# Graph layer: one unit in 60 fetched row by row on SyncE's queue

## The chip, the cores and the metric

The kernel runs on one core of a Trainium2 chip. The time is the device time of that core in microseconds, the median of three runs: 16161.78 us (16160.94 to 16164.18). Times in the profile come from one profiled execution of the same program, times of single instructions in nanoseconds where marked.

## The reference

A layer of a graph network on N = 50,000 nodes with 160 features (64 scalars and 32 vectors of 3) and 1,650,000 edges. The edges come sorted by destination. Each edge has a source, a destination and four numbers sh.

```
ss, vv = s[src], v[src]                       # rows of x, gathered by source
dot  = einsum('eui,ei->eu', vv, e1)           # e0 = sh[:, 0:1], e1 = sh[:, 1:4]
out0 = C0 * (ss * e0 @ W1 + dot * INV3 @ W2)
out1 = C1 * (p3 + p4 + p5)                    # products of ss, vv, cross(vv, e1) with e0, e1, W3, W4, W5
m_agg = segment_sum(concat(out0, out1), dst)  # summed over the edges of a destination
h    = m_agg's two parts @ Ws, Wv             # scaled
x    = layernorm(x + (x + relu(h)))
```

All of it is linear in the gathered row up to the relu. So the kernel sums, for each destination and each of the four numbers, (number x gathered row) first, and applies one combined weight matrix of 4 x 160 by 160 afterwards.

## The kernel before

The edges are cut into units of 128 edges: 12,891 of them, 12,894 with the padding. Six units are a group (G = 6): its destinations fit into a window of 32 slots (W = 32). There are 2149 groups. Two groups are a pair (PG = 2, 12 units), four groups a chunk whose 4 x 32 slots fill 128 partitions, and 20 groups a super-chunk (SG = 20, 120 units, 10 pairs); there are 108 super-chunks, the last with 9 groups.

`load` (L186 to L206) fetches a super-chunk's indices `ri` and edge numbers `ra` on SyncE's (SP's) queue at L193, L194 and L195, one unit to a partition. ScalarE (ACT) turns the indices into floats at L197, TensorE (PE) transposes them (L200, L205) so that an edge is on its own partition, and VectorE (DVE) writes the sources back as integers `si` (L202). `place` (L208 to L217) subtracts each group's first destination. Loads are made one super-chunk ahead.

`group_sums` (L219 to L242) handles a pair. GpSimd (POOL) issues one indirect DMA per unit, L225: 128 rows of x of 640 bytes each, one to a partition, into a part of the tile `xg`; 12 such parts make a tile, and there are 8 tiles (`rows`, bufs=8). DVE makes one-hot matrices times edge numbers (`hot` L230, `ha` L233). PE multiplies `ha` with the gathered rows, six units accumulating into one group's sums `ps` (L238), and ACT copies `ps` to `A` (L241).

`apply_weights` (L244 to L268) transposes a chunk's sums (L253), multiplies with the weights (L263) and leaves the rows `hp` (L267). `block` (L270 to L287) collects the chunks that touch a block of 128 nodes: SP loads the block's own rows `xt` (L275, 3 buffers), ACT doubles them (L277), PE gathers the chunks with a one-hot matrix (L286), and `norm` (L143 to L156) does relu, residual and layer norm and stores `out` on ACT's queue (L156). There are 391 blocks.

The main loop (L318 to L334) goes over the pairs: a load of the next super-chunk at the first pair of one, `group_sums`, then the chunk and the blocks that became complete a pair ago. Each engine works its own queue in order; the tile framework sets that order and puts in the waits, and a buffer of a pool is given out again when its last reader is done. What follows the loop checks that the windows held all edges, and a second path after it (L372 on, loops of zero turns on these inputs) would redo the work otherwise.

Of the kernel before, what the change touches and what calls it, by code (L numbers as in the profile page):

```python
# [29 lines left out]

F32 = mybir.dt.float32
I32 = mybir.dt.int32
AF = mybir.ActivationFunctionType
ALU = mybir.AluOpType
AX = mybir.AxisListType
ET = mybir.EngineType
PSUM = bass.MemoryType.PSUM

P = 128
MUL0, MUL1 = 64, 32  # L40
D = MUL0 + 3 * MUL1
# [10 lines left out]
QG = P // W  # L52
PG = 2
SG = 20


def plan(n_nodes, n_edges):

    nblk = 125
    assert n_nodes % nblk == 0  # L60
    nb = n_nodes // nblk
    again = 9

    per_unit = P * n_nodes / n_edges
    group = max(g for g in range(1, 17)
                if g == 1 or g * per_unit + 1 + 5 * math.sqrt(g * per_unit * per_unit / P) <= W)
    ngroups = math.ceil(math.ceil(n_edges / P) / group)
    units = P * math.ceil(max(math.ceil(n_edges / P) + again - 1, QG * math.ceil(ngroups / QG) * group) / P)
    return nblk, nb, again, group, units, ngroups
# [3 lines left out]
def tile_gnn_resnorm(ctx: ExitStack, tc: tile.TileContext, x, src, dst, attr, W1, W2, W3, W4, W5, Ws, Wv, out, n_edges):  # L73
    nc = tc.nc
    N = x.shape[0]
    NBLK, NB, GA, G, NU, NG = plan(N, n_edges)
# [14 lines left out]
    BWb = const.tile([D - P, NK, D], F32, name="BWb")  # L91
    more = const.tile([1, 2], I32, name="more")

    src1 = src.rearrange("(e o) -> e o", o=1)
    dst1 = dst.rearrange("(e o) -> e o", o=1)

    def weights(wp, psum):
# [45 lines left out]
    def norm(pool, ph, x2, n, row):  # L143
# [7 lines left out]
        rstd = pool.tile([P, 1], F32, name="rstd")  # L151
        nc.scalar.activation(rstd[:n], mv[:n, 1:2], AF.Sqrt, bias=eps_t[:n])  # L152
        nc.vector.reciprocal(rstd[:n], rstd[:n])  # L153
# [15 lines left out]
    alive = max(bs[-1] - bs[0] for bs in of_block) + 1  # L169
    NSC = math.ceil(NG / SG)  # L170

    with tc.tile_pool(name="once", bufs=1) as once, tc.tile_pool(name="raw", bufs=2) as rawp, \
            tc.tile_pool(name="idx", bufs=2) as idxp, tc.tile_pool(name="rows", bufs=8) as rowp, \
            tc.tile_pool(name="ops", bufs=3) as op, tc.tile_pool(name="sums", bufs=4) as sump, \
            tc.tile_pool(name="hp", bufs=alive + 3) as hpp, tc.tile_pool(name="node", bufs=3) as np_, \
            tc.tile_pool(name="psC", bufs=1, space=PSUM) as psC, tc.tile_pool(name="psK", bufs=2, space=PSUM) as psK, \
# [9 lines left out]
        def load(s):  # L186

            n = (min(NG, (s + 1) * SG) - s * SG) * G
            u0 = s * SG * G
            e = slice(u0 * P, (u0 + n) * P)  # L190
            ri = rawp.tile([P, 2, P], I32, name="ri")
            ra = rawp.tile([P, P, NK], F32, name="ra")
            nc.sync.dma_start(ri[:n, 0, :], src1[e].rearrange("(u p) o -> u (p o)", p=P))  # L193
            nc.sync.dma_start(ri[:n, 1, :], dst1[e].rearrange("(u p) o -> u (p o)", p=P))  # L194
            nc.sync.dma_start(ra[:n].rearrange("u p k -> u (p k)"), attr[e].rearrange("(u p) k -> u (p k)", p=P))  # L195
            rf = rawp.tile([P, 2, P], F32, name="rf")
            nc.scalar.copy(rf[:n], ri[:n])  # L197
            pi = psI.tile([P, 2, P], F32, name="pi")
            for i in range(2):
                nc.tensor.transpose(pi[:, i, :n], rf[:n, i, :], ident[:n, :n])  # L200
            si = idxp.tile([P, P], I32, name="si")
            nc.vector.tensor_copy(si[:, :n], pi[:, 0, :n])  # L202
            pk = psK.tile([P, NK, P], F32, name="pk")
            for k in range(NK):
                nc.tensor.transpose(pk[:, k, :n], ra[:n, :, k], ident[:n, :n])  # L205
            return s, n, si, pi, pk  # L206

        def place(loaded):  # L208

            s, n, si, pi, pk = loaded  # L210
            rel = idxp.tile([P, P], F32, name="rel")
            nc.vector.tensor_tensor(
                rel[:, :n].rearrange("p (g j) -> p g j", j=G), pi[:, 1, :n].rearrange("p (g j) -> p g j", j=G),
                baseB[:, s * SG:s * SG + n // G].unsqueeze(2).to_broadcast([P, n // G, G]), op=ALU.subtract)
            nc.vector.tensor_reduce(extremes[:, 0, s:s + 1], rel[:, :n], axis=AX.X, op=ALU.min)
            nc.vector.tensor_reduce(extremes[:, 1, s:s + 1], rel[:, :n], axis=AX.X, op=ALU.max)
            return si, rel, pk  # L217

        def group_sums(placed, u, ng):  # L219

            si, rel, pk = placed
            n = ng * G
            xg = rowp.tile([P, PG * G, D], F32, name="xg")
            for j in range(n):
                nc.gpsimd.indirect_dma_start(  # L225
                    out=xg[:, j, :], out_offset=None, in_=x,
                    in_offset=bass.IndirectOffsetOnAxis(ap=si[:, u + j:u + j + 1], axis=0))

            hot = op.tile([P, PG * G, W], F32, name="hot")
            nc.vector.tensor_tensor(hot[:, :n], slotsP[:, 0:W].unsqueeze(1).to_broadcast([P, n, W]),  # L230
                                    rel[:, u:u + n].unsqueeze(2).to_broadcast([P, n, W]), op=ALU.is_equal)
            ha = op.tile([P, PG * G, NK, W], F32, name="ha")
            nc.vector.tensor_tensor(ha[:, :n], hot[:, :n].unsqueeze(2).to_broadcast([P, n, NK, W]),  # L233
                                    pk[:, :, u:u + n].rearrange("p k u -> p u k").unsqueeze(3)
                                    .to_broadcast([P, n, NK, W]), op=ALU.mult)
            ps = psA.tile([P, PG, D], F32, name="ps")
            for j in range(n):
                nc.tensor.matmul(ps[:, j // G, :], ha[:, j].rearrange("p k w -> p (k w)"), xg[:, j, :],  # L238
                                 start=j % G == 0, stop=j % G == G - 1)
            A = sump.tile([P, PG, D], F32, name="A")  # L240
            nc.scalar.copy(A[:, :ng], ps[:, :ng])  # L241
            return A, ng  # L242

        def apply_weights(pairs):  # L244
# [3 lines left out]
            for f0, f1 in ((0, P), (P, D)):  # L248
                pt = psM.tile([P, QG, P], F32, name="pt", tag="misc")
                g = 0  # L250
                for A, n in pairs:
                    for i in range(n):
                        nc.tensor.transpose(pt[:f1 - f0, g, :], A[:, i, f0:f1], ident)  # L253
                        g += 1
# [15 lines left out]
        def block(b, hps):  # L270
# [15 lines left out]
                nc.tensor.matmul(ph[:nb], hot2[:r, i, :nb], hp[:r], start=i == 0, stop=i == len(cs) - 1)  # L286
            norm(np_, ph[:nb], x2[:nb], nb, row)  # L287

        loaded = {0: load(0)}


        base_d = dram.tile([NGP, 1], I32, name="base_d")
        with nc.allow_non_contiguous_dma(reason="one number of each group"):
            nc.sync.dma_start(base_d, dst1[0:NGP * G * P].rearrange("(g e) o -> g (e o)", e=G * P)[:, 0:1])
        baseI = once.tile([P, NGP], I32, name="baseI")
        nc.sync.dma_start(baseI, base_d.rearrange("g o -> o g").to_broadcast([P, NGP]))
# [3 lines left out]
        for g in range(QG):  # L300
            r = slice(g * W, (g + 1) * W)
# [4 lines left out]
        placed = {0: place(loaded.pop(0))}  # L306
# [10 lines left out]
        g = 0  # L317
        while g < NG:  # L318
            s = g // SG
            if g % SG == 0 and s + 1 < NSC:  # L320
                loaded[s + 1] = load(s + 1)
            ng = min(PG, NG - g, (s + 1) * SG - g)
            got = group_sums(placed[s], (g - s * SG) * G, ng)
            if ready:
                second(*ready.pop())
            pairs.append(got)
            g += ng
            if g % QG == 0 or g == NG:
                ready.append((c, pairs))
                pairs, c = [], c + 1  # L330
            if g % SG == 0 and g < NG:
                placed[s + 1] = place(loaded.pop(s + 1))
                del placed[s]
# [3 lines left out]
        far = once.tile([P, NCH], F32, name="far")  # L337
# [25 lines left out]
    mm_d = dram.tile([2, NU], F32, name="mm_d")  # L363
    tab_d = dram.tile([2, NB], I32, name="tab_d")
    tab = const.tile([1, 2, NB], I32, name="tab")
# [7 lines left out]
    with tc.tile_pool(name="up", bufs=1) as up, tc.tile_pool(name="us", bufs=2) as us, tc.For_i(0, once_more, 1):  # L373
# [16 lines left out]
        far = up.tile([PB, 2, CB, nseg], F32, name="far2")  # L390
        for s in range(nseg):
# [7 lines left out]
            for c in range(CB):  # L399
# [3 lines left out]
                at = us.tile([PB, 2, SEG], F32, name="at")  # L403
# [5 lines left out]
        f = up.tile([PB, CB], F32, name="f")  # L409
# [12 lines left out]
    with tc.tile_pool(name="edges2", bufs=2) as ep, tc.tile_pool(name="ops2", bufs=2) as op, \  # L422
# [3 lines left out]
        with tc.For_i(0, blocks, 1) as b:  # L426
# [5 lines left out]
            with tc.For_i(u0, u1, GA) as u:  # L432
                u = nc.s_assert_within(u, 0, NU - GA, skip_runtime_bounds_check_because="below u1")
# [9 lines left out]
                xg = op.tile([P, GA, D], F32, name="xg2")  # L443
# [10 lines left out]
                ps = psA.tile([NBLK, 2, 512], F32, name="ps2")  # L454
# [7 lines left out]
            for f0, f1 in ((0, P), (P, D)):  # L462
# [3 lines left out]
                at = np_.tile([f1 - f0, NK, NBLK], F32, name=f"ac{f0}")  # L466
# [3 lines left out]
            i = 0  # L470
# [4 lines left out]
            row = ds(b * NBLK, NBLK)  # L475
# [37 lines left out]
```

## Time and profile before

| what | value |
|---|---|
| median of three runs | 16161.78 us |
| the profiled execution's own time | 16161.21 us |
| its span, first to last instruction | 16159.5 us |
| granted TensorE clock | 0.662 |
| gathers (L225) | 12894, 945 ns each |
| gathers' DMA queue | 618912 packets, 1057.10 MB, 26.6% of the 16 DMA engines |
| SP's DMA queue | 102084 packets, 72.77 MB, 1.6% |
| issue of `xt` on SP (L275), min/median/max | 327/351/616 ns, 1.9 us to landing |
| issue of `ri` (L193, L194) and `ra` (L195), median | 347, 403 and 347 ns |
| CAST of the indices on ACT (L197) | 398 ns |
| load of one register on SP (TENSOR_LOAD, L359), two of them | 290 and 475 ns |

"Busy" is the time in which an engine executes instructions; register, semaphore and DMA-issuing instructions are left out of it, so SP has no row. "Idle before, releaser" tells what the engine waited for ahead of an instruction; "issue" means that it waited for nothing that the profile shows. The time of a DMA instruction on SP is the time in which SP is occupied with it, and "to landing" runs from the issue to the arrival of the data.

### The profile page before, as it was taken

How to read it: one execution, taken by the hardware profiler on the slowest of the kernel's cores; microseconds unless marked ns; L12 is line 12 of the kernel's file. 1: busy time of each engine (PE TensorE's matmuls, PEld its weight loads, DVE VectorE, ACT ScalarE, POOL GpSimd, SP SyncE). 2: the span in 40 equal slices, each digit the busy share in tenths (PEclk: the TensorE clock that was granted, in tenths of full speed). 3: DMA queues.
4: the chain of work that ended last, by engine and by line, in shares of the span. 5: the costliest groups of instructions: out<-in, count | busy, mean ns of one | idle time of the engine just before them, and what ended most of it. 6: DMA issues, size and time to landing. Idle time of an engine off the chain costs nothing. (4 is left out here: it accounts for less than half of the span.)

```text
span 16159.5 us, 115933 instructions
## 1 busy us (share of the span) xinstructions
PE 13061.2 (81%) x43943; PEld 9172.6 (57%) x43944; DVE 3450.3 (21%) x5361; ACT 1521.6 (9%) x3583; POOL 12192.5 (75%) x12905
## 2 busy tenths in 40 slices
PE   7878888878888887888888888888788888887887
PEld 5555555555555555555555555555555555555555
DVE  2222222222222222222222222222222222222221
ACT  1000000000000000000000000000000000000000
POOL 7777777777777777777777777777777777777776
PEclk6666666666666666666666666666666666666666
DMA  3222222222222222222222222222222222222222
GB/s 79 73 72 72 73 73 72 72 73 72 72 73 72 72 73 73 72 73 72 73 72 73 72 73 72 73 72 72 73 72 73 72 72 72 73 73 72 72 71 65
DMA packets 778423, 1169.89 MB, mean 72 GB/s; under 512 B 226314, under 2 KB 558406, under 8 KB 777732
## 3 DMA queue, kind: packets, MB, share of 16 engines
q0 software_dynamic: 618912, 1057.10, 26.6%
q1 hardware_dynamic: 102084, 72.77, 1.6%
q10 hardware_dynamic: 56864, 32.58, 0.7%
q8 instruction: 346, 5.67, 0.1%
q14 instruction: 217, 1.78, 0.0%
HBM read 1129.30 MB, written 32.25 MB: 72 GB/s over the span
## 5 line engine op out<-in xcount | busy, mean ns | idle before, releaser
L225 POOL DMA_INDIRECT xg<-in_x,si x12894 | 12190.9, 945 | 3933.3 <-issue 3793.9
L238 PE MATMUL ps<-xg,ha 128*128 128x160 f32 x25788 | 8965.8, 457 | 3056.3 <-DMA xg<-in_x,si 2998.2
L238 PEld LDWEIGHTS ps<-xg,ha 128*128 128x128 f32 x25788 | 5534.5, 267 | 6130.7 <-DMA xg<-in_x,si 5458.9
L233 DVE TENSOR_TENSOR ha<-hot,pk 128x1536 f32<-128x1536 f32 x1075 | 1884.7, 1753 | 10801.5 <-PE ps L238 10801.5
L263 PE MATMUL phc<-BWb,at 32*128 32x160 f32 x4304 | 1624.9, 471 | 0.0
L241 ACT COPY A<-ps 128x320 f32<-128x320 f32 x1075 | 456.8, 425 | 11583.8 <-PE ps L238 11569.5
L253 PE MATMUL pt<-ident,A 128*128 128x128 f32 x4298 | 1361.4, 394 | 0.4 <-ACT at L256 0.4
L286 PE MATMUL phb<-hp,hot 128*128 128x160 f32 x4584 | 1349.4, 483 | 0.0
L286 PEld LDWEIGHTS phb<-hp,hot 128*128 128x128 f32 x4584 | 1202.2, 331 | 129.0 <-issue 129.0
L263 PE MATMUL phc<-BWa,at 128*128 128x160 f32 x4304 | 1262.7, 386 | 0.0
L263 PEld LDWEIGHTS phc<-BWb,at 32*128 32x128 f32 x4304 | 892.6, 256 | 557.2 <-issue 556.7
L263 PEld LDWEIGHTS phc<-BWa,at 128*128 128x128 f32 x4304 | 1026.0, 270 | 0.4 <-DVE st L148 0.2
L253 PEld LDWEIGHTS pt<-ident,A 128*128 128x128 f32 x4298 | 750.1, 175 | 104.8 <-ACT at L256 0.8
L256 ACT COPY at<-pt 128x512 f32<-128x512 f32 (+1 forms) x1076 | 623.2, 579 | 1137.6 <-PE pt L253 1137.4
L230 DVE TENSOR_TENSOR hot<-slotsP,rel 128x384 f32<-128x384 f32 x1075 | 597.0, 556 | 31.4
L281 DVE TENSOR_TENSOR hot<-slotsP,rr 128x768 f32<-128x768 f32 (+2 forms) x391 | 362.9, 928 | 0.0
L146 DVE SCALAR_TENSOR_TENSOR y<-phb,x 128x160 f32<-128x160 f32 x391 | 126.9, 325 | 800.3 <-PE phb L286 800.3
L277 ACT ACTIVATE x<-xt 128x160 f32<-128x160 f32 x391 | 131.6, 337 | 1341.7 <-DVE y L146 1341.2
L202 DVE CAST si<-pi 128x120 int32<-128x120 f32 x108 | 30.4, 282 | 882.9 <-DMA xg<-in_x,si 879.7
L267 ACT COPY hp<-phc 128x160 f32<-128x160 f32 x538 | 157.3, 292 | 195.0 <-PE phc L263 194.9
L155 DVE TENSOR_SCALAR o<-y,mv,rstd 128x160 f32<-128x160 f32 x391 | 149.2, 382 | 14.1
L152 ACT ACTIVATE rstd<-mv,eps_t 128x1 f32<-128x1 f32 x391 | 115.2, 295 | 334.3 <-DVE mv L150 329.6
(67 smaller groups left out, 856.0 us busy)
## 6 DMA issues: line engine op xcount, KB each, us to landing
xg<-in_x,si POOLq DMA_INDIRECT x12894, 2.6
xt<-in_x SPq DMA_DIRECT2D x390, 80.0 KB, 1.9
out<-o ACTq DMA_DIRECT2D x390, 80.0 KB, 1.7
ra<-in_attr SPq DMA_DIRECT2D x107, 240.0 KB, 3.0
ri<-in_src SPq DMA_DIRECT2D x107, 60.0 KB, 2.0
ri<-in_dst SPq DMA_DIRECT2D x107, 60.0 KB, 2.0
baseI<-base_d SPq DMA_DIRECT2D x1, 1076.0 KB, 7.5
BVd<-BV ACTq DMA_DIRECT2D x1, 240.0 KB
```

Of the source, the lines that this page charges most:

```text
L155: nc.vector.tensor_scalar(o[:n], y[:n], mv[:n, 0:1], rstd[:n], op0=ALU.subtract, op1=ALU.mult)
L225: nc.gpsimd.indirect_dma_start(out=xg[:, j, :], out_offset=None, in_=x, in_offset=bass.IndirectOffsetOnAxis(ap=si[:, u + j:u + j + 1], axi ...
L230: nc.vector.tensor_tensor(hot[:, :n], slotsP[:, 0:W].unsqueeze(1).to_broadcast([P, n, W]), rel[:, u:u + n].unsqueeze(2).to_broadcast([P, n ...
L233: nc.vector.tensor_tensor(ha[:, :n], hot[:, :n].unsqueeze(2).to_broadcast([P, n, NK, W]), pk[:, :, u:u + n].rearrange("p k u -> p u k").un ...
L238: nc.tensor.matmul(ps[:, j // G, :], ha[:, j].rearrange("p k w -> p (k w)"), xg[:, j, :], start=j % G == 0, stop=j % G == G - 1)
L241: nc.scalar.copy(A[:, :ng], ps[:, :ng])
L253: nc.tensor.transpose(pt[:f1 - f0, g, :], A[:, i, f0:f1], ident)
L256: nc.scalar.copy(at[:, :, :ng].rearrange("f k g w -> f g k w"), pt[:f1 - f0, :ng].rearrange("f g (k w) -> f g k w", w=W))
L263: nc.tensor.matmul(ph[:ng * W], at[:, k, :ng].rearrange("f g w -> f (g w)"), bw[:, k, :], start=i == 0, stop=i == 2 * NK - 1)
L267: nc.scalar.copy(hp[:ng * W], ph[:ng * W])
L281: nc.vector.tensor_tensor(hot2[:, :len(cs)], slotsP.unsqueeze(1).to_broadcast([P, len(cs), P]), rr[:, :len(cs)].unsqueeze(2).to_broadcast( ...
L286: nc.tensor.matmul(ph[:nb], hot2[:r, i, :nb], hp[:r], start=i == 0, stop=i == len(cs) - 1)
```

## The change

In pairs 4 and 9 of each super-chunk the twelfth unit is no longer gathered by POOL. Its 128 rows are fetched by SP with 128 DMAs of one row each, into a tile `xr` of its own (a pool of 3 buffers). For the addresses ACT makes a tile `ro` of byte offsets (source x 640) from the loaded indices, still one unit to a partition, and SP reads 32 of them at a time into registers. The rows of a unit are issued in four steps of 32: one step is placed at each of the four pairs ahead of the one that uses them. The matmul of that unit reads `xr` in place of `xg`. A pair is left alone if its number over all is below 4 or if it doesn't lie fully within the groups.

```diff
+HELP = {ET.SP: (4, 9)}
+ROWS = 32
...
+    xbytes = x.bitcast(U8).rearrange("n f -> (n f)")
...
+            tc.tile_pool(name="far", bufs=3) as farp, \
...
+            ro = rawp.tile([P, P], I32, name="ro")
+            nc.scalar.mul(ro[:n], ri[:n, 0, :], 4.0 * D)
+            offsets[s] = ro
...
-        def group_sums(placed, u, ng):
+        def group_sums(placed, u, ng, q):
...
-            for j in range(n):
+            xr = fetched.pop(q, None)
+            for j in range(n - (xr is not None)):
                 nc.gpsimd.indirect_dma_start(
...
-                nc.tensor.matmul(ps[:, j // G, :], ha[:, j].rearrange("p k w -> p (k w)"), xg[:, j, :],
+                nc.tensor.matmul(ps[:, j // G, :], ha[:, j].rearrange("p k w -> p (k w)"),
+                                 xr if xr is not None and j == n - 1 else xg[:, j, :],
                                  start=j % G == 0, stop=j % G == G - 1)
+            for eng in HELP:
+                fetch(q, eng)
...
+        queues = {ET.SP: nc.sync, ET.Activation: nc.scalar}
+        offsets, fetched = {}, {}
+        ppair = SG // PG
+        steps = P // ROWS
+        todo = {}
+        for s in range(NSC):
+            for eng, at in HELP.items():
+                for m in at:
+                    q = s * ppair + m
+                    if q >= steps and (s * SG + (m + 1) * PG) <= NG:
+                        for i in range(steps):
+                            todo.setdefault((q - steps + i, eng), []).append((q, s, (m + 1) * PG * G - 1, i))
+
+        def fetch(q, eng):
+
+            for q1, s, u, i in todo.pop((q, eng), []):
+                if i == 0:
+                    fetched[q1] = farp.tile([P, D], F32, name=f"xr{list(HELP).index(eng)}")
+                xr = fetched[q1]
+                _, at = nc.values_load_multi_w_load_instructions(
+                    offsets[s][u:u + 1, i * ROWS:(i + 1) * ROWS], engines=[eng], min_val=0, max_val=(N - 1) * 4 * D,
+                    skip_runtime_bounds_check_because="an offset of a row of x")
+                for j, v in enumerate(at):
+                    r = i * ROWS + j
+                    queues[eng].dma_start(xr[r:r + 1, :].bitcast(U8),
+                                          xbytes[ds(v, 4 * D)].rearrange("(o f) -> o f", o=1))
...
-            got = group_sums(placed[s], (g - s * SG) * G, ng)
+            got = group_sums(placed[s], (g - s * SG) * G, ng, s * ppair + (g - s * SG) // PG)
```

More of the change, by code (lines that the diff above doesn't have):

```diff
@@ L32 @@
 I32 = mybir.dt.int32
+U8 = mybir.dt.uint8
 AF = mybir.ActivationFunctionType
```

## The prediction

> **What bounds the kernel now.** I read the page's first part, then its groups, then the order of time in one stretch, then SyncE's (SP's) own waits. First the busy shares, then three groups (columns: busy us, mean ns of one, idle before it and its releaser):
>
> ```profile
> PE 13061.2 (81%) x43943; PEld 9172.6 (57%) x43944; DVE 3450.3 (21%) x5361; ACT 1521.6 (9%) x3583; POOL 12192.5 (75%) x12905
> ...
> L225 POOL DMA_INDIRECT xg<-in_x,si x12894 | 12190.9, 945 | 3933.3 <-issue 3793.9
> L238 PE MATMUL ps<-xg,ha 128*128 128x160 f32 x25788 | 8965.8, 457 | 3056.3 <-DMA xg<-in_x,si 2998.2
> ```
>
> PE looks busiest, but its idle time ends on the gathers' data (2998.2 us), while POOL's ends on "issue": it waits for nobody. The timeline shows the beat (start, duration):
>
> ```profile
> 8009.65 0.95 POOL L225 DMA_INDIRECT xg<-in_x,si  x1 [0.30 <-issue]
> ...
> 8010.90 0.95 POOL L225 DMA_INDIRECT xg<-in_x,si  x1 [0.30 <-issue]
> ...
> 8012.15 0.95 POOL L225 DMA_INDIRECT xg<-in_x,si  x1 [0.30 <-issue]
> ```
>
> One gather every 1.25 us: 0.95 busy, 0.30 between two. First and last gather start at 7.5 and 16125.5 us, so (16125.5 - 7.5)/12893 = 1.2501 us, from end to end. POOL's "75%" is a full queue. The kernel is 12894 beats (16119 us), 7.5 us ahead and 33 us behind.
>
> SP's waits show what SP has free (us in total, times, longest), and its timeline what one transfer costs it:
>
> ```profile
> SPq L275 <- ACT x L277: 11989.5, 385, 87.0
> SPq L193 <- ACT rf L197: 2044.9, 104, 36.7
> SPq L195 <- PE pk L205: 1593.7, 104, 31.8
> ```
>
> ```profile
> 15016.29 0.35 SPq L193 DMA_DIRECT2D ri<-in_src  x1
> 15016.69 0.40 SPq L194 DMA_DIRECT2D ri<-in_dst  x1
> ```
>
> 15628 of 16160 us are waits for a buffer to come free: SP is idle, and runs ahead. One transfer occupies SP for 0.35 us, the next follows at 0.40.
>
> **What the Trainium skill says.** "Perfetto Trace Analysis", DMA Instruction — HWDGE: the profiled duration is the sequencer's own time (lock, descriptors, semaphore), not the movement. So 0.35 us is SP's price, and it hardly depends on size here: 60 KB and 240 KB both take 347 ns. "DMA: Bandwidth & Descriptors", Issuing engines are not separate DMA queues: a second issuer saves sequencer time and nothing of the transfer. That is what is scarce: the gathers' queue fills 26.6% of the 16 engines. "Runtime: NRT & Kernel Launch", Instruction fetch mechanics: a register load costs about 200 ns per register, even in bulk. The trace has only loads of one register on SP, 290 and 475 ns.
>
> **The change part by part.** *Removed.* The last gather of pairs 4 and 9 in each super-chunk of 20 groups (120 units). Of 108 super-chunks the last, with 9 groups, has neither: 107 x 2 = 214 gathers. 214 x 1.2501 = 267.5 us off POOL's queue. A super-chunk falls from 120 x 1.2501 = 150.0 to 118 x 1.2501 = 147.5 us.
>
> *Added on SP.* Per fetched unit 128 transfers of one row (640 B) and 4 loads of 32 registers; per super-chunk 256 transfers and 8 loads, beside 3 loads of indices and attributes and 391/108 = 3.6 of xt, at 0.42 us each 2.8 us. SP must end this within 147.5 us. With r for a row and l for a load: T = 256 r + 8 l + 2.8.
>
> r isn't in the trace (one row, address in a register). From below: 0.327 us, the fastest xt. From above: 0.60 us, the dearest of the ordinary small transfers (the weight loads on ACT, 0.472 to 0.604). I take 0.45: 0.35, the gap of 0.05 that 0.40 start to start leaves, and 0.05, an estimate, for the register address. The view of x is in bytes, so the loaded number is the address and no arithmetic stands between.
> l: from below 0.29 us, if 32 registers cost one trip; from above 32 x 0.2 = 6.4 us, an estimate by the skill's price. I take 2.0[...], which nothing here shows.
> T = 115.2 + 16 + 2.8 = 134 us, 91% of 147.5. Both low: 89 us. Both high: 153.6 + 51.2 + 2.8 = 208 us. SP keeps up while r < (147.5 - 18.8)/256 = 0.503 us; break-even with before is r = (150.0 - 18.8)/256 = 0.512 us. The margin over my 0.45 is 0.05 to 0.06 us a row: this decides the case.
>
> *Moved past.* Behind the rows on SP stand xt (ACT waits for it, L277), and ri and ra of the next super-chunk (ACT at L197, PE at L205). They now start up to one batch of 32 rows late, 32 x 0.45 + 2 = 16 us; all are issued far ahead (SP waits up to 87 us for the buffer of xt), so nothing if SP keeps its lead. If that lead is gone, ACT waits and everything behind it.
>
> *Added waits.* The first row of a unit waits until PE has read that buffer three fetched units before: about 15 pairs, 220 us ago, nothing. A load waits for ACT's new offsets, made with the chunk's load: nothing. PE's last matmul of pairs 4 and 9 waits for the rows; behind it on PE are the next pairs. A late row isn't lost at once: xg has 8 buffers, so POOL can be some 7 pairs (105 us) ahead before it stops, and PE gains on it (13061/1075 = 12.1 us busy per pair against 14.75). A load's eight completion semaphores cost PE a few waits of 0.05 us (the EVENT_SEMAPHORE rows): 214 x 0.4 = 86 us in all, inside its 3056 us of idle.
>
> *Added on ACT.* One multiplication of 120x128 per super-chunk, about 0.4 us by the CAST at L197 (398 ns), 108 x 0.4 = 43 us on an engine busy 9%: hidden, and 43 us if it weren't.
>
> *The DMA engines.* 27392 rows. At 40.5 ns a packet (1.6% of 16 x 16159.5 us over 102084 packets of SP's queue), with one data and one semaphore packet 2.2 ms of engine time. On one engine alone that is 14% of the span beside its 27 to 30%; in 16 pieces over 16 engines the same 14% on each. Room either way, and POOL's beat is descriptor work that doesn't wait for them.
>
> *Sum.* Profiled execution 16161.2 us (span 16159.5), median 16161.8, 0.6 us apart, so one subtraction serves both: 16161.8 - 267.5 = 15894.3 us, -1.66%. Below it I see nothing beyond some 15 us of luck at the ends.
>
> **Rivals.** Outside the 107 super-chunks with help lie 16161.8 - 107 x 150.0 = 112 us; where SP binds the time is 112 + 107 T.
>
> (1) *SP becomes the bound: slower.* If a row costs over 0.512 us with l = 2.0, or l is over 4.0 with r = 0.45, SP's queue outlasts what POOL saves. With l at the skill's price T = 115.2 + 51.2 + 2.8 = 169.2: 18216 us (+13%). With r = 0.60, l = 2.0: T = 172.4, 18559 us. Both: 22370 us. For it: no register-addressed transfer and no bulk load is in the trace, and the margin is a tenth. Against it: 0.35 us is steady over 700 issues of three sizes.
>
> (2) *SP and ACT in lock-step: a part is lost.* In the program of before, the transfers of SP and ACT share eight completion semaphores in turn, and each waits for the one eight before it. With 70 rows between two of ACT's out transfers, ACT's out waits for SP's rows and SP's next row for ACT's out. With 3.6 outs per super-chunk, 4 us lost by SP at each makes T = 134 + 14.5 = 148.5, 1 us over POOL's: 107 x 1 = 107 us back, 16001 us. For it: the EVENT_SEMAPHORE ahead of 314 of 391 out transfers. Against: 13.5 us of slack per super-chunk takes most of it.
>
> (3) *No gain.* POOL's beat lengthens as POOL and SP load the same engines; 2 beats in 120 is 21 ns per gather. 16162 us. For it: gathers and rows read the same memory. Against: the beat is 1.25 us throughout, whatever else moves.
>
> **How the numbers follow.** Forecast 0.57, lock-step 0.07, no gain 0.03, SP the bound 0.33. 0.2% is about what a measurement of this kernel can tell from no change. Faster 0.64, same 0.03, slower 0.33. The likeliest time is 15894, its own range 15880 to 15930. For 8 in 10 the first three cases (0.67) need 0.13 of the slower one: up to T = 157.8, a row at 0.543 us with l = 2.0 or a load at 5.0 us with r = 0.45, which is 112 + 107 x 157.8 = 16997. Range 15880 to 17000; 0.20 of the slower case lies beyond.
>
> **What would show it.** Right: 12680 gathers, still 1.25 us apart with idle on "issue"; row transfers of 0.33 to 0.45 us on SP, loads near 2 us, and SP still waiting for L277's and L197's successors, some 13 us per super-chunk. Wrong: POOL's idle ends on PE (a full xg), PE's on the row tile, SP is without waits and T is read from its rows; or ACT's out transfers wait for a DMA of SP. A longer beat on POOL would be rival 3.

## The result, and the profile after

The changed kernel takes 15898.24 us (15896.68 to 15901.16), the kernel before in the same runs 16161.47 us: a ratio of 0.9837 with a 95% interval of 0.982 to 0.9854. Forecast were 15894 us and 1.66% less; it is 263 us and 1.63%.

The page of the changed kernel, busy shares and the groups that answer to those shown of before (the gather is now L236, the matmuls L249):

```profile
PE 8954.0 (56%) x43943; PEld 7314.3 (46%) x43944; DVE 3435.1 (22%) x5361; ACT 1481.1 (9%) x3691; POOL 11991.2 (75%) x12691
...
L236 POOL DMA_INDIRECT xg<-in_x,si x12680 | 11989.6, 946 | 3871.5 <-issue 3720.3
L249 PE MATMUL ps<-xg,ha 128*128 128x160 f32 x25360 | 5635.9, 365 | 1456.6 <-DMA xg<-in_x,si 1377.1
...
L249 PE MATMUL ps<-xr,ha 128*128 128x160 f32 x428 | 186.2, 539 | 5118.5 <-DMA xr<-in_x 3795.1
```

12680 gathers, and GpSimd (POOL) still waits for nobody ("issue"). The views of the gather's line, before and after, give the durations in ns (min/median/max) and the first and last start:

```profile
L225 POOL DMA_INDIRECT xg<-in_x,si x12894: 940/946/1101, 7.5 to 16125.5; - x199
L236 POOL DMA_INDIRECT xg<-in_x,si x12680: 942/946/1422, 7.0 to 15862.3; - x199
```

(15862.3 - 7.0)/12679 = 1.2505 us a beat, 1.2501 before. The time is still the beats plus both ends. TensorE (PE) is another matter: it now waits for the fetched rows, 3795 us in total. Counted from the end of a pair's last gather to the start of ACT's copy of its sums, PE is late by 24.3 us in the median and by 57.6 at most, after 2.7 and 19.0 in the kernel before.

What a row and a load of 32 registers cost SyncE (SP), from the views of the tiles `xr` and `ro` (duration in ns, min/median/max). The MOVE is a register instruction that stands ahead of each row's transfer:

```profile
L328 SPq MOVE xr<-in_x x27392: 29/29/38, 21.5 to 15839.7; - x200
L328 SPq DMA_DIRECT2D xr<-in_x x27392: 227/228/403, 21.6 to 15839.8; - x200
```

```profile
L323 SPq TENSOR_LOAD <-ro x856: 2080/2177/2380, 19.3 to 15827.0; - x172
```

And SP's timeline, in which 27 rows without a wait between them take 8.63 us, (8.63 - 0.228)/26 = 0.323 us from start to start:

```profile
8000.06 8.63 SPq L328 DMA_DIRECT2D xr<-in_x  x27
8008.78 0.37 SPq L289 DMA_DIRECT2D xt<-in_x  x1
8009.20 0.42 SPq L199 DMA_DIRECT2D ri<-in_src  x1
```

From the start of a load to that of the next instruction it takes 2.24 us on average. SP's own sum for a super-chunk is 256 x 0.323 + 8 x 2.24 + 3.4 (the other transfers, their waits' instructions) = 104 us of 147.5, where 134 were forecast.

SP's waits in the changed kernel (us in total, times, longest), and two of all engines' waits:

```profile
SPq L328 <- DMA out<-o: 4484.7, 386, 67.3
SPq L323 <- ACT rf L203: 119.6, 62, 2.4
SPq L323 <- ACT A L255: 66.3, 34, 2.3
```

```profile
ACT x L291 <- DMA xt<-in_x: 4876.1, 285, 39.2
...
PE ps L249 <- DMA xr<-in_x: 3795.1, 148, 34.2
```

ACT's doubling of `xt`, before and after:

```profile
L277 ACT ACTIVATE x<-xt 128x160 f32<-128x160 f32 x391 | 131.6, 337 | 1341.7 <-DVE y L146 1341.2
L291 ACT ACTIVATE x<-xt 128x160 f32<-128x160 f32 x391 | 131.4, 336 | 4878.0 <-DMA xt<-in_x 4876.1
```

Before, SP waited for buffers and was far ahead. Now it waits 386 times for one of ScalarE's (ACT's) out transfers, 42 us a super-chunk, and ACT in turn waits for `xt`, which stands behind the rows on SP. In the trace the same eight semaphores carry SP's transfers and ACT's. That is the lock-step of rival 2, and larger than it was priced. The waits fill time that SP has to spare (104 + 42 is just about 147.5); what they cost is measured below, and it is little.

### The profile page after: what moved, and what is told of

It reads as the page before. It is cut to its first block, busy times and chain, and to the rows that moved or that the text cites. A ratio compares the mean times of both kernels' runs of the same rounds, so it can differ in the third digit from the quotient of the medians.

```text
span 15896.2 us, 172106 instructions
## 1 busy us (share of the span) xinstructions
PE 8954.0 (56%) x43943; PEld 7314.3 (46%) x43944; DVE 3435.1 (22%) x5361; ACT 1481.1 (9%) x3691; POOL 11991.2 (75%) x12691
## 3 DMA queue, kind: packets, MB, share of 16 engines
q0 software_dynamic: 608640, 1039.56, 24.6%
q1 hardware_dynamic: 156868, 90.41, 2.2%
## 5 line engine op out<-in xcount | busy, mean ns | idle before, releaser
L236 POOL DMA_INDIRECT xg<-in_x,si x12680 | 11989.6, 946 | 3871.5 <-issue 3720.3
L249 PE MATMUL ps<-xg,ha 128*128 128x160 f32 x25360 | 5635.9, 365 | 1456.6 <-DMA xg<-in_x,si 1377.1
L249 PEld LDWEIGHTS ps<-xg,ha 128*128 128x128 f32 x25360 | 4356.0, 226 | 2578.2 <-DMA xg<-in_x,si 2297.7
L249 PE MATMUL ps<-xr,ha 128*128 128x160 f32 x428 | 186.2, 539 | 5118.5 <-DMA xr<-in_x 3795.1
L249 PEld LDWEIGHTS ps<-xr,ha 128*128 128x128 f32 x428 | 107.5, 312 | 5186.1 <-issue 2723.7
L267 PE MATMUL pt<-ident,A 128*128 128x128 f32 (+1 forms) x4298 | 866.8, 338 | 264.1 <-DVE y L151 246.8
L277 PE MATMUL phc<-BWa,at 128*128 128x160 f32 x4304 | 939.6, 376 | 18.1 <-ACT at L270 14.6
L277 PEld LDWEIGHTS phc<-BWa,at 128*128 128x128 f32 x4304 | 833.3, 250 | 87.8 <-ACT at L270 69.1
L277 PE MATMUL phc<-BWb,at 32*128 32x160 f32 x4304 | 847.5, 343 | 0.0
L300 PE MATMUL phb<-hp,hot 128*128 128x160 f32 x4584 | 799.2, 329 | 7.3 <-ACT hp L281 7.3
L267 PEld LDWEIGHTS pt<-ident,A 128*128 128x128 f32 (+1 forms) x4298 | 566.8, 146 | 408.5 <-DVE y L151 309.1
L300 PEld LDWEIGHTS phb<-hp,hot 128*128 128x128 f32 x4584 | 717.0, 210 | 61.0 <-issue 47.6
```

Of the source, the lines that this page charges most:

```text
L236: nc.gpsimd.indirect_dma_start(out=xg[:, j, :], out_offset=None, in_=x, in_offset=bass.IndirectOffsetOnAxis(ap=si[:, u + j:u + j + 1], axi ...
L277: nc.tensor.matmul(ph[:ng * W], at[:, k, :ng].rearrange("f g w -> f (g w)"), bw[:, k, :], start=i == 0, stop=i == 2 * NK - 1)
```

## Experiments

Of the first five kernels below, four ran with the kernel before at 16163.66 us, and "one unit" with it at 16162.44. The others ran on three chips on which the kernel before itself takes 18354 to 18455 us, called the second kind here, so their times are read only against that.

**The gathers stay, the rows are fetched as well.**

```diff
-            for j in range(n - (xr is not None)):
+            for j in range(n):
```

> The rows are fetched on SP and used, and the gathers that they replace are issued as well, into a part of xg that is then not read. Theory (GpSimd's queue of 1.25 us beats is the only bound; SP's work, the rows' traffic and their waits are hidden): 12894 beats again, 16161 us. Rival (the gain comes from elsewhere, such as the looser order of TensorE or its clock of 0.676 after 0.662): well below 16161, towards 15900. Rival (the fetch has a price that the removed gathers overpaid): above 16161.

Measured: 16169.27 us, ratio to before 1.0003 (0.9994 to 1.0012). The gather's line:

```profile
L236 POOL DMA_INDIRECT xg<-in_x,si x12894: 942/947/1250, 7.0 to 16137.9; - x199
```

The whole gain is gone, and nothing but the 214 gathers came back. PE's looser order, its waits (3892 us for rows), its higher granted clock (0.672 after 0.660) and SP's rows are all there, and the time is that of before to within the interval. So the gain is the beats, and neither the rows' traffic nor the order helps or hurts beyond some 6 us. (In the profiled execution, the slowest of the twelve at 16174.3 us, the last gather starts 12 us later than before, a beat longer by 1 ns.)

**Neither gathered nor fetched.** The 214 units' own rows are left out of the sums.

```diff
-            xr = fetched.pop(q, None)
+            xr = left.pop(q, None)
...
-                                 xr if xr is not None and j == n - 1 else xg[:, j, :],
+                                 xg[:, j - (j == n - 1 and xr is not None), :],
...
-            for eng in HELP:
-                fetch(q, eng)
...
+        left = {}
...
+                        left[q] = True
```

(`left`, and so `xr`, here only marks that the unit is one of the 214. Its matmul reads the unit before it a second time.)

> Neither gathered nor fetched: the 214 units' own rows are left out, their matmul reads the unit before it a second time, and ACT still makes the offsets. Theory (the fetch is fully hidden): 12680 beats, 15894 us, within 5 us of the changed kernel's 15898. Rival (the fetch costs part of the gain, by waits or by traffic): 15850 or less here.

Measured: 15895.34 us, ratio 0.9834 (0.9817 to 0.985). That is 268.3 us less than before, the 267.5 us of 214 beats. It is 2.9 us less than the changed kernel, or 5.1 if each is taken against the kernel before of its own runs. So the fetch of 27392 rows, with the lock-step, costs some 3 to 5 us in all. SP's waits in this kernel show where its lead went in the other:

```profile
SPq L287 <- ACT x L289: 12016.8, 387, 84.0
SPq L199 <- ACT rf L203: 1778.8, 103, 31.4
```

Without rows SP waits for buffers as before the change, for up to 84 us; the wait for out transfers is absent.

**One unit in a super-chunk.**

```diff
-HELP = {ET.SP: (4, 9)}
+HELP = {ET.SP: (4,)}
```

> One unit of each super-chunk on SP (pair 4), 107 in all. On a chip where the kernel before takes some 16161 us: 107 x 1.2501 us less, 16028 us, half of the changed kernel's gain. On a chip like that of the two runs before (kernel before 18361 us; there a row took SP 0.82 us from start to start, SP's sum was about 228 us a super-chunk and filled the span): theory (SP's sum is the bound there, nothing else of the change): half of the rows need 128 x 0.82 + 4 x 2 + 4 = 117 us, well below 18361/107 = 172 us, so the time falls back to the kernel before's or below, 18100 to 18400 us. Rival (that chip is slow by the number of instructions of all engines, 115933 in 18361 us before, some 172000 in 24563 us): some 144000 instructions at 143 to 158 ns, 20600 to 22800 us.

Measured: 16032.93 us, ratio 0.992 (0.9903 to 0.9936), 129.5 us less than before for 107 beats of 1.2501 us, 133.8. The gain goes with the number of gathers removed; again some 4 us are missing. SP's sum is about half here, and its waits for out transfers are 10020 us.

**Three units in a super-chunk.**

```diff
-HELP = {ET.SP: (4, 9)}
+HELP = {ET.SP: (3, 6, 9)}
```

> Three units of each super-chunk on SP (pairs 3, 6 and 9), 320 in all, instead of two. From the changed kernel's trace a row takes SP 0.323 us from start to start and a load of 32 registers 2.24 us, so SP needs 384 x 0.323 + 12 x 2.24 + 3.4 = 154.3 us a super-chunk, against 117 x 1.2501 = 146.3 us on GpSimd. Theory (SP becomes the bound where its sum passes GpSimd's): 112 + 107 x 154.3 = 16620 us, more if SP also loses time waiting for ACT's out transfers (in the changed kernel 42 us a super-chunk): with all of it, 112 + 107 x 196 = 21100 us. Rival (GpSimd stays the bound, SP overlaps more than its sum says): 16161 - 320 x 1.2501 = 15761 us.

Measured: 18246.54 us, ratio 1.1288 (1.1269 to 1.1307). By the rule 112 + 107 T that is T = 169.5 us a super-chunk. The waits of SP, and of GpSimd and TensorE:

```profile
SPq L328 <- DMA out<-o: 1380.8, 387, 66.2
SPq L323 <- ACT x L291: 119.4, 62, 2.2
```

```profile
PE ps L249 <- DMA xr<-in_x: 9019.6, 311, 44.0
...
POOL xg L236 <- PE ps L249: 2122.4, 277, 18.3
```

GpSimd now stops for a buffer of xg that PE hasn't released, and PE waits for rows: SP is the bound, as rival 1 put it, only at another number of rows. SP's sum was to be 154.3 us, which alone makes 16620 us; it also waits 1380.8/107 = 12.9 us for out transfers and 1.1 us for the loads, together 168.3. So where SP binds, the lock-step seems no longer free: its waits add 8% to SP's sum. That the 13 us would go if the out transfers didn't share semaphores with SP's was to be tested (further down) and isn't shown.

**Four buffers of xg.**

```diff
-            tc.tile_pool(name="idx", bufs=2) as idxp, tc.tile_pool(name="rows", bufs=8) as rowp, \
+            tc.tile_pool(name="idx", bufs=2) as idxp, tc.tile_pool(name="rows", bufs=4) as rowp, \
```

> The changed kernel with 4 buffers of xg instead of 8. In its trace the copy of a pair's sums comes up to 57 us after the pair's last gather (2.7 us before the change), some 3.8 pairs. Theory (SP and ACT hold each other up through the shared semaphores, TensorE gets the rows late, and only the 8 buffers of xg keep this from GpSimd): with 4 buffers GpSimd can be about 3 pairs, 44 us, ahead, and loses some 10 us at one or two pairs of a super-chunk: 16200 to 17500 us, with GpSimd's idle time ended by PE. Rival (the lateness is harmless because the order gives way): 15900 us.

Measured: 15898.73 us, ratio 0.9837 (0.982 to 0.9853): a miss of the theory as it was written. The waits:

```profile
PE ps L249 <- DMA xr<-in_x: 3843.0, 149, 34.7
POOL xg L236 <- issue: 3737.7, 12262, 0.3
```

PE's lateness is as in the changed kernel, median 24.5 us, at most 57.8, and GpSimd doesn't feel it. The likely reason is one that the working had left out: PE waits at the pair's last matmul, when the 11 gathered units have been read and the buffer can be given out again; four buffers then hold four pairs, 4 x 14.75 = 59 us, just above the largest lateness. Whether fewer would fail is what the next kernel was to show.

**Three buffers of xg**, which by that account don't hold it (`bufs=3` in the same place). It ran twice, with the same expectation:

> The changed kernel with 3 buffers of xg. With 4 nothing was lost: where TensorE waits for a fetched unit it has already read the other 11 of the pair, so that pair's buffer is free, and 4 buffers hold 4 pairs, 59 us, against at most 57.6 us of lateness. Theory (the lateness is real and hidden by the buffers alone): 3 buffers hold 44 us, the copies of pairs 4 and 9 come 53 and 47 us late, so GpSimd stops for some 9 and 3 us in each super-chunk: 15898 + 107 x 12 = 17180 us, somewhat less if the lateness shrinks by what GpSimd lost; GpSimd's idle time then ends on PE. Rival (the lateness gives way, since SP has a third of its time to spare): 15900 to 15950 us.

> The changed kernel with 3 buffers of xg, again (the first time the kernel before took 18381 us on that chip). With 4 nothing was lost: where TensorE waits for a fetched unit it has already read the other 11 of the pair, so that pair's buffer is free, and 4 buffers hold 4 pairs, 59 us, against at most 57.6 us of lateness. Theory (the lateness is real and hidden by the buffers alone): 3 buffers hold 44 us, the copies of pairs 4 and 9 come 53 and 47 us late, so GpSimd stops for some 9 and 3 us in each super-chunk: 15898 + 107 x 12 = 17180 us, somewhat less if the lateness shrinks by what GpSimd lost; GpSimd's idle time then ends on PE. Rival (the lateness gives way, since SP has a third of its time to spare): 15900 to 15950 us.

Measured: 24537.25 and 24562.91 us, where the kernel before took 18380.85 and 18361.33: ratios 1.3338 (1.3303 to 1.3372) and 1.3359 (1.3319 to 1.34). SP's rows (second run), and what ended most of GpSimd's idle time (us, times):

```profile
L328 SPq MOVE xr<-in_x x27392: 1/29/1399, 22.4 to 24581.3; - x200
L328 SPq DMA_DIRECT2D xr<-in_x x27392: 1/228/1402, 22.5 to 24581.3; - x200
```

```profile
  PE ps L249: 8624.8, 532
```

The medians are those of the other chip, but many instructions of SP last some 0.7 us, or twice that: 7533 of 57017 in the first of these runs lie between 0.66 and 0.73 us, and none in the changed kernel's own trace. From the start of its MOVE to that of the next instruction, waits included, a row takes SP 0.819 us on average, against 0.495 in the changed kernel. Most of those 0.495 us beyond 0.323 are waits for out transfers (4485 us in all); here the listed waits are fewer, 1333 us for out transfers and 299 for earlier rows, and without them a row still takes 0.76 us. 256 x 0.76 alone is 195 us a super-chunk, well above GpSimd's 147.5. So SP's queue can't keep up there, which is the picture of rival 1, and with the waits, the loads and the rest it fills the span of some 24600 us. GpSimd's 0.946 us, the 1.251 us from gather to gather in the median, and PE's median matmul of 299 ns are not longer there. What the third buffer would have cost is lost in this: the question of the buffers stays open below four.

**Two and three units in turn**, the version that the sums pointed to:

```diff
-                for m in at:
+                for m in ((3, 6, 9) if s % 2 else at):
```

> Two units on SP in even super-chunks, three in odd ones (267 in all). SP's sum is 104 and 154 us, 129 on average, GpSimd's beats take 147.5 and 146.3, 146.9 on average; with three units everywhere SP lost another 15 us a super-chunk, which makes 137 to 144 here. Theory (the sum over two super-chunks counts, the buffers carry the difference): 16161 - 267 x 1.2501 = 15828 us, faster than the changed kernel. Rival (each odd super-chunk is bound by itself): 53 x (169.5 - 147) = 1190 us more, 17020 us.

> Again: two units on SP in even super-chunks, three in odd ones (267 or 268 in all). SP's sum is 104 and 154 us, 129 on average, GpSimd's beats take 147.5 and 146.3, 146.9 on average; with three units everywhere SP lost another 15 us a super-chunk, which makes 137 to 144 here. Theory (the sum over two super-chunks counts, the buffers carry the difference): 16161 - 267 x 1.2501 = 15828 us, faster than the changed kernel. Rival (each odd super-chunk is bound by itself): 53 x (169.5 - 147) = 1190 us more, 17020 us.

> Once more, in the hope of the first chip's conditions (kernel before 16162 us): two units on SP in even super-chunks, three in odd ones. Theory (the sum over two super-chunks counts: SP 129 to 144 us against GpSimd's 146.9): 268 x 1.2501 us less than 16162, 15827 us, faster than the changed kernel. Rival (each odd super-chunk is bound by itself, at 169.5 us): 17020 us; between the two if TensorE's lateness of an odd super-chunk, some 23 us more, is only in part worked off in the even one that follows.

Measured: 26408.68, 26444.56 and 26417.98 us, with the kernel before at 18380.85, 18361.33 and 18387.89: ratios 1.4351, 1.4381 and 1.4366 (the last 1.4327 to 1.4405). All three runs met chips of the second kind, so whether it reaches 15827 us on the first kind isn't known. In the third trace 34304 rows take SP 0.694 us each, 23812 us in all, of which the listed waits are 1334 us for out transfers and 316 for earlier rows: SP's own work fills most of the span again.

**Rows on ACT's queue as well.**

```diff
-HELP = {ET.SP: (4, 9)}
+HELP = {ET.SP: (4, 9), ET.Activation: (2, 7)}
```

> ACT fetches one unit in 60 as well (pairs 2 and 7), SP as in the changed kernel: 428 gathers less. ACT's added work is 256 x 0.323 + 8 x 2.24 = 101 us a super-chunk beside its 14 us of busy time and 1 us of out transfers, 116 us, and SP's is 104; GpSimd's beats are 116 x 1.2501 = 145.0. Theory (only sums count): 112 + 107 x 145.0 = 15627 us. Rival (lock-step: ACT's queue also carries the copies that TensorE and VectorE wait for, so that rows hold up the rows' own consumers): slower than the changed kernel, 16500 us and more, with TensorE and VectorE waiting for ACT.

Measured: 22611.78 us, before 18380.85, ratio 1.23 (1.2267 to 1.2333). The waits:

```profile
ACT A L255 <- DMA xr<-in_x: 12627.5, 721, 41.3
DVE ha L244 <- PE ps L249: 10771.0, 659, 50.2
PEld pt L267 <- ACT A L255: 5320.5, 326, 22.3
```

ACT's copy of the sums waits for rows that are in flight, and PE's transposes for that copy. This speaks for the rival, rows holding up their own consumers; its size on the first kind of chip isn't known. The time is below that of the kernels in which SP alone carried the rows there, although its program has the most instructions (227783), so the number of instructions of all engines isn't what sets the time on these chips.

**Three units, out transfers on GpSimd's queue.**

```diff
-HELP = {ET.SP: (4, 9)}
+HELP = {ET.SP: (3, 6, 9)}
...
-        nc.scalar.dma_start(out[row, :], o[:n])
+        nc.gpsimd.dma_start(out[row, :], o[:n])
```

> Three units on SP, with the out transfers issued by GpSimd, whose completion semaphores are others than those that SP and ACT share. Theory (of the 169.5 us a super-chunk that three units took, 154.3 are SP's own sum and the rest is SP waiting for ACT's out transfers): 112 + 107 x 154.3 = 16620 us; GpSimd has 146.3 + 3.6 x 1.25 = 150.9 us and isn't the bound. Rival (the rest comes from something else, such as the loads' waits or TensorE's order): 18250 us as before.

Measured: 26965.55 us, before 18380.85, ratio 1.4663 (1.4625 to 1.47), on such a chip again. SP's waits for out transfers are gone from its list, as the edit intends, but 41088 rows take 0.581 us each, counted as above (0.365 in the three-unit kernel on the first kind of chip), and nothing can be said of the 13 us.

## Why the prediction was right

*What bounds the kernel, and the removal.* Right: 214 beats fewer, worth 267.5 us by the sum, 268.3 when nothing is put in their place, 263.2 in the changed kernel. The 4 us short are a beat longer by 0.4 ns, 12680 times, less 0.6 us at the ends.

*SP's sum.* Right in its verdict, with two terms mis-sized, and in part lucky: neither price was in the trace, and the margin of 0.05 to 0.06 us a row was smaller than the error of the estimate. A row's r was taken as 0.45 us and is 0.323; the floor of 0.327, the fastest issue of a 128-row transfer, was no floor, since a transfer of one row is issued in 0.228 us. An instruction was missed: each register-addressed transfer has a MOVE of 29 ns ahead of it. A load's l was taken as 2.0 us and is 2.18, far below the 6.4 us of the upper end, which came from the price per register of the Trainium skill ("Runtime: NRT & Kernel Launch", Instruction fetch mechanics); here it is 68 ns a register. So T is 104 us and not 134, and the break-even lies near r = 0.51 us as written, with a margin of 0.18 where 0.06 was seen.

*Rival 1.* Wrong for two units, and shown as a mechanism with three: there the formula's 154.3 us pass GpSimd's 146.3 and the time rises to 18247 us, more than the formula's 16620. The second kind of chip fits it: a row takes 0.76 us without the listed waits, above 0.512, and the version with three buffers takes 24.5 ms; but the changed kernel itself never ran there, and the kernel before is slower there too. Its chance of 0.33 stood on an unknown price; the price was on the good side on the chip of the result. On the second kind no version ran faster than the kernel before.

*Rival 2, and what is queued behind the rows.* The mechanism was named and is there, but two statements on it failed. The lead that was to hide xt is gone: ACT waits 4876 us for xt, and SP 42 us a super-chunk for out transfers where 14.5 were priced. And the 107 us that it was to cost are 3 to 5, since SP had 43 us to spare and xg's buffers cover a lateness of up to 57.6 us. Eight buffers were called a cover of seven pairs; four buffers are enough. Of the signs, then, the gathers and the loads came as listed under "right", but SP's waits of 13 us for the old buffers did not, and PE's wait for the row tile, listed under "wrong", came with a right time: the sign that counts is GpSimd's, which still waits for nobody.

*Rival 3.* Not seen: with rows and all gathers together a beat is 1.2511 us (16130.9/12893) against 1.2501.

*The DMA engines.* SP's queue rose from 102084 to 156868 packets, by 54784 = 2 x 27392: two packets a row, as the estimate took. The gathers' queue fills 24.6% of the engines after 26.6%, but 26.6% with the same 12680 gathers and four buffers, so nothing follows from that.

## What to carry to other kernels

When one queue issues at a fixed beat and waits for nobody, the gain of taking work from it is the count times the beat, and an idle queue can take that work as long as its own sum per period stays below. Write that sum and its break-even down before anything else, because beyond it the loss is soon larger than the gain (two units gained 1.6%, three lost 12.9%). Count the waits that tie two queues together, here completion semaphores shared in turn by SP and ACT: they were nearly free while there was slack (42 us of waits, at most 5 us lost in all) and seem to add to the sum once there is none (12.9 us of 169.5, not isolated). A kernel that puts many small instructions on a queue depends on their price on the chip at hand (0.32 us a row on one kind of chip here, 0.76 on another).

## What was not expected

- One row of 640 bytes with its address in a register is issued on SP in 228 ns (0.323 us from start to start with its MOVE), less than the 327 to 351 ns (fastest and median) of a transfer of 128 rows in the kernel before.
- A load of 32 registers takes 2.18 us, 68 ns a register, while a load of one takes 290 or 475 ns.
- PE's matmuls on the gathered rows got shorter, 457 to 365 ns on average, and its busy time fell from 13061 to 8954 us with the same instructions. The likely reason is that PE, being late, finds its data there and doesn't meet each gather one by one: the busy time falls with the lateness, to 11344 us with one unit and 7387 with three, and it is 12890 with nothing fetched. None of it shows in the time, since PE isn't the bound.
- On three of the five chips of the experiments the kernel before took 18.35 to 18.46 ms, and in the kernels with rows SP's instructions were drawn out to 0.7 us many times. Why is open; no trace of the kernel before exists from there.
